# Nine-tap depthwise convolutions of a windowed-attention layer: one part of each on GpSimd instead of VectorE

## The chip, the cores and the metric

The kernel runs on one core of a Trainium2 chip. The metric is the device time of one execution in microseconds (us), from the first to the last instruction plus what lies around it. Its engines work side by side, each with its own queue of instructions in order: TensorE (PE; its weight loads are listed as PEld), VectorE (DVE), ScalarE (ACT), GpSimd (POOL) and SyncE (SP), which issues the DMAs. They wait for each other by semaphores.

## The reference

Four layers in a row, each on an image batch of 4 x 192 x 56 x 56 in float32: a convolutional attention with an MLP, a channel gate from a DCT pooling, a windowed attention with overlapping windows, and a four-direction selective scan. The change is in the third one. After its attention it computes:

```python
def _hft(x, w, b):
    a = 3.0 * x
    for s in (2, 4, 8):
        pool = x.reshape(B, C, h // s, s, ww // s, s).mean(axis=(3, 5))
        a = a - jnp.repeat(jnp.repeat(pool, s, axis=2), s, axis=3)
    return jax.nn.sigmoid(_dwconv3(a, w, b)) * x

out = _hft(_conv1x1(out, proj_w, proj_b), hft_w, hft_b)
x1 = x + out
z = jax.nn.gelu(_conv1x1(_ln_c(x1, n2g, n2b), fc1_w, fc1_b), approximate=False)
z1, z2 = jnp.split(z, 2, axis=1)
z = z1 * _dwconv3(_ln_c(z2, sgn_g, sgn_b), sg_w, sg_b)
return x1 + _conv1x1(z, fc2_w, fc2_b)
```

`_dwconv3` is a depthwise 3x3 convolution with a border of zeros: every channel with nine weights of its own. The first (the gate) has 192 channels, the second (in the MLP) 384.

## The kernel before, in words

Channels lie on partitions: 192 as two halves of 96, 384 as three parts of 128. In the third layer (`layer2` in the code) each image is cut in two ways. The attention goes by five bands of rows: `front` (layer norm, q and k), 25 `quad`s of four windows in each band (GpSimd copies the windows out into `xw` and `qw` at L1737, TensorE multiplies, VectorE adds the bias, finds the maximum and subtracts it, ScalarE takes the exponential, and VectorE adds the results into the accumulator `bacc` at L1841), and `back` (division and projection into `bp`). What follows the attention goes by seven chunks of eight rows, 28 in all. Chunk i passes through three threads of work:

- `head(i)`: VectorE makes the sums over 2, 4 and 8 pixels and the padded image `bapad`, then the gate's convolution into `bxn` (`dwconv`, L1527 the first tap with the bias, L1529 the other eight, for two halves); ScalarE a tanh (L1596), GpSimd copies two rows of `bapad` on for the next chunk (L1597), VectorE multiplies and adds (L1600, L1602), then a layer norm.
- `grow(i)`: GpSimd copies two rows of `bzpad` (L1647), TensorE expands to 768 channels, ScalarE applies the GELU; the half z2 is normed into the padded image `bzpad`, the half z1 stays in `bz`.
- `tail(i)`: the MLP's convolution of `bzpad` into `bg` (`dwconv` again, for three parts), VectorE's product with z1 (L1683), GpSimd's copy of a row of z1 (L1684), the last projection (L1692) and the sum into `bp` (L1700).

A chunk has 7 to 9 rows in `head` (7, 8, 8, 8, 8, 8, 9 in an image) and 6 to 10 in `tail` (6, 8, 8, 8, 8, 8, 10); a row is 56 pixels. So a tap of an eight-row chunk is one VectorE instruction of 448 elements for each half or part, which reads the shifted window of the padded image and the sum so far, and writes the sum.

The order of the work on PE, DVE, ACT and POOL is made while the program is built, by the class `Order`. Every thread is a generator that yields the engine and the estimated cost of its next step (`on_dve`, `on_pool` and so on, with a microsecond formula each), or a condition that must hold first. Of all threads whose next step may go, `Order.run` takes the one that could start first, with 0.05 us for each unit of the thread's place as a handicap. The outcome is one fixed queue for each engine; at run time, semaphores alone make an engine wait. A buffer kind named in `Order` is taken by `take` and given back by `done`. `gone(...)` and the `at` counters are the conditions: `head(i)` begins when `head(i - 1)` is through, `tail(i)` when `tail(i - 1)` is, `grow(i)` when the convolution of `tail(i - 2)` is.

Before the layer, the second layer's last gate scales image 3 in 14 pieces, each loaded into a buffer `xg`, scaled by ScalarE and stored again (L1184 to L1191); two such buffers exist. `front` of image 3 waits until that is over.

Of the kernel before, what the change touches and what calls it, by code (L numbers as in the profile page):

```python
# [15 lines left out]
F32 = mybir.dt.float32  # L16
AF = mybir.ActivationFunctionType
ALU = mybir.AluOpType
# [4 lines left out]
B, C, H, W = 4, 192, 56, 56  # L23
HW = H * W
HALF = 96
CH = 448
# [235 lines left out]
class Order:  # L262
# [29 lines left out]
    def take(self, kind="bank"):  # L292
        slot = min((s for s in self.kinds[kind] if s[0] is not None), key=lambda s: s[0])
        slot[0] = None
        return slot[1]
# [71 lines left out]
def on_dve(*n, takes=(), ready=None, each=0.00105):  # L367
    return "DVE", sum(0.08 + each * i for i in n), takes, None, ready
# [10 lines left out]
def on_pool(*n, each=0.0011):  # L379
    return "POOL", sum(0.2 + each * i for i in n), (), None, None  # L380


def on_sp(*takes):
    return "SP", 0.5, takes, None, None


BASE2, BASE3 = 150, 330
# [24 lines left out]
def layers01(tc, pools, x_in, packs, aps, dst):  # L412
    nc = tc.nc
# [6 lines left out]
    last = pools["2"].enter_context(tc.tile_pool(name="a_last", bufs=1, side="right"))  # L420
# [14 lines left out]
    with tc.tile_pool(name="a_stat", bufs=6) as sp:  # L435
# [3 lines left out]
        for b in range(B):  # L439
            for c in range(NCHUNK):  # L440
                t = sp.tile([HALF, 2, CH], F32, name="xs")
# [99 lines left out]
    def keep(name, shape, n, rows=128, pool=per):  # L541
        return [pool.tile([rows, *shape], F32, name=f"{name}{i}") for i in range(n)]

    def keep_att(*args):
        return keep(*args, pool=att)
# [15 lines left out]
    for t in bank_tiles:  # L561
        nc.vector.memset(t, 0.0)
    order = Order(
        nc,
        bank=bank_tiles,
        xc=xc,
        xq=xq,
        vt=keep_att("vt", [NG, 4, 64], 1, 112),
        X=keep_att("X", [WIN, 2, PADW], 4),
        sm=keep_att("sm", [WIN, W], 4),  # L570
        sd=keep_att("sd", [WIN, W], 1),
# [1 line left out]
        vb=keep_att("vb", [7, 256], 2, 112),  # L573
        ot=keep("ot", [14 * 112], 4),
        pool=keep("pool", [2, H * DCT], 1, HALF),
        xg=keep("xg", [CH], 2, HALF, last),
        hm=keep("hm", [CH], 2),
    )
    take, done = order.take, order.done
# [217 lines left out]
    parts = ((0, 16), (16, 28))  # L797
# [436 lines left out]
def layer2(tc, order, pools, src, packs, aps, dst):  # L1234
# [9 lines left out]
    nc = tc.nc  # L1244
# [11 lines left out]
    def keep(name, shape, n, rows=128):  # L1256
        return [const.tile([rows, *shape], F32, name=f"{name}{i}") for i in range(n)]
# [86 lines left out]
    p2 = ctx.enter_context(tc.tile_pool(name="b_2", bufs=1, side="right"))  # L1344
# [62 lines left out]
    def gone(*what):  # L1407
        return what[-1] < 0 or what in passed
# [107 lines left out]
                done(po)  # L1516
        at["back"] += 1

    def dwconv(parts):


        for t in range(9):
            yield on_dve(*(n * W for _, _, _, n, _, _ in parts), each=0.0012)
            for dst, pad, i, n, wt, bias in parts:
                x = pad[:, i + t // 3 : i + t // 3 + n, t % 3 : t % 3 + W]
                if t == 0:
                    nc.vector.tensor_scalar(dst, x, wt[:, 0:1], bias, ALU.mult, ALU.add)  # L1527
                else:
                    nc.vector.scalar_tensor_tensor(dst, x, wt[:, t : t + 1], dst, ALU.mult, ALU.add)  # L1529

    def rows_behind(c, n):

        return max(8 * c - n, 0), (H if c == NCHUNK - 1 else 8 * c + 8 - n)
# [3 lines left out]
    def head(i):  # L1537

        b, c = divmod(i, NCHUNK)
        y0, y1 = rows_behind(c, 1)  # L1540
        n = y1 - y0
        xn = xn2s[i % 2]
        yield lambda: at["head"] == i and at["back"] > NB * b + band_of[c] and gone("z1", i - 2)
        yield on_sp("xl")
        xt = take("xl")
        xr = xt[:HALF, :, : n * W]
        nc.sync.dma_start(xr, pixels(src[b])[:, :, y0 * W : y1 * W])

        x = pr[:HALF, :, 8 * c : 8 * c + 8]
        sums = []  # L1550
        for m in (4, 2, 1):
            xs = 7 * m
            yield on_dve(2 * m * xs, 2 * m * xs, m * xs, m * xs)
            a = p2.tile([HALF, 2, 2 * m, xs], F32, name=f"hx{m}", tag=f"hx{m}", bufs=1)
            v = x.rearrange("p h y (x r) -> p h y x r", r=2)
            for h in range(2):
                nc.vector.tensor_add(a[:, h], v[:, h, :, :, 0], v[:, h, :, :, 1])
            s = p2.tile([HALF, 2, m, xs], F32, name=f"hs{m}", tag=f"hs{m}", bufs=1)
            v = a.rearrange("p h (y r) x -> p h y r x", r=2)
            for h in range(2):  # L1560
                nc.vector.tensor_add(s[:, h], v[:, h, :, 0], v[:, h, :, 1])
            sums.append(s)
            x = s
        s2, s4, s8 = sums
        for t, u, m in ((s4, s8, 1), (s2, s4, 2)):
            yield on_dve(*[14 * m * m] * 4)
            for i_ in range(2):
                for h in range(2):
                    tv = t[:, h].rearrange("p (y r) (x s) -> p r y x s", r=2, s=2)[:, i_]
                    nc.vector.scalar_tensor_tensor(tv, bcast(u[:, h], 3, 2), 0.25, tv, ALU.mult, ALU.add)  # L1570
        yield on_dve(*[224] * 4)
        if c == 0:
            nc.gpsimd.memset(apad[:, :, 1, 1 : 1 + W], 0.0)
        for i_ in range(2):
            for h in range(2):

                out = apad[:, h, 2 + i_ : 10 : 2, 1 : 1 + W].rearrange("p y (x s) -> p y x s", s=2)
                v = pr[:HALF, h, 8 * c + i_ : 8 * c + 8 : 2].rearrange("p y (x s) -> p y x s", s=2)
                nc.vector.scalar_tensor_tensor(out, bcast(s2[:, h], 3, 2), -1.0 / 12, v, ALU.mult, ALU.add)
        gate = xn[:HALF, :, : n * W]  # L1580
        yield from dwconv(
            [
                (
                    rows2(gate[:, h]),
                    apad[:, h],
                    y0 + 1 - 8 * c,
                    n,
                    w["b96.hft_w"][:, h],
                    w["b96.hft_b"][:, h : h + 1],
                )  # L1590
                for h in range(2)
            ]
        )

        yield on_act(2 * n * W, table=GELU)
        nc.scalar.activation(gate, gate, AF.Tanh, scale=0.5)  # L1596
        nc.gpsimd.tensor_copy(apad[:, :, 0:2, 1 : 1 + W], apad[:, :, 8:10, 1 : 1 + W])  # L1597
        px = slice(y0 * W, y1 * W)
        yield on_dve(2 * n * W)
        nc.vector.scalar_tensor_tensor(gate, gate, 1.0, p[:HALF, :, px], ALU.add, ALU.mult)  # L1600
        yield on_dve(2 * n * W)
        nc.vector.scalar_tensor_tensor(p[:HALF, :, px], gate, 0.5, xr, ALU.mult, ALU.add)  # L1602
        done(xt)
        yield from layer_norm(p[:, :, px], xn[:, :, : n * W], n * W, HALF, 2, mean96)
        at["head"] += 1
# [60 lines left out]
    def tail(i):  # L1666

        b, c = divmod(i, NCHUNK)
        zpad = zpads[i % 2]
        yield lambda: at["tail"] == i and gone("z2", i)  # L1670
        y0, y1 = rows_behind(c, 2)
        n = y1 - y0
        i1 = y0 + 2 - 8 * c
        yield from dwconv(
            [
                (g[:, m, :n], zpad[:, m], i1, n, w["b128.sg_w"][:, m], w["b128.sg_b"][:, m : m + 1])
                for m in range(3)
            ]
        )
        passed.add(("conv", i))  # L1680
        yield lambda: gone("z1", i)
        yield on_dve(3 * n * W)
        nc.vector.tensor_mul(g[:, :, :n], g[:, :, :n], z1[:, :, i1 : i1 + n])  # L1683
        nc.gpsimd.tensor_copy(z1[:, :, 0], z1[:, :, 8])  # L1684
        passed.add(("product", i))
        for u, v in ((0, n),) if n <= 8 else ((0, n // 2), (n // 2, n)):
            px = slice((y0 + u) * W, (y0 + v) * W)
            for h in range(2):
                yield on_pe(3 * (v - u) * W, "bank")
                po = take()  # L1690
                for m in range(3):
                    nc.tensor.matmul(  # L1692
                        rows2(po[:HALF, : (v - u) * W]),
                        w["b128.fc2T"][:, m, HALF * h : HALF * h + HALF],
                        g[:, m, u:v],
                        start=(m == 0),
                        stop=(m == 2),
                    )
                yield on_dve((v - u) * W)
                nc.vector.scalar_tensor_tensor(  # L1700
                    p[:HALF, h, px],
                    po[:HALF, : (v - u) * W],
                    w["b96.fc2_b"][:, h : h + 1],
                    p[:HALF, h, px],
                    ALU.add,
                    ALU.add,
                )
                done(po)
            yield on_sp()
            nc.sync.dma_start(pixels(dst[b])[:, :, px], p[:HALF, :, px])  # L1710
        at["tail"] += 1
# [701 lines left out]
```

## Time and profile before

| what | before |
|---|---|
| runs | 5952.47, 5952.52, 5965.42 us; median 5952.52 |
| profiled execution | 5975.54 us |
| its span, first to last instruction | 5973.8 us |
| mean granted TensorE clock | 0.926 |
| PE busy | 4964.2 us (83%) |
| DVE busy | 4435.9 us (74%) |
| ACT busy | 2574.0 us (43%) |
| POOL busy | 1475.0 us (25%) |
| DMA, mean | 79 GB/s |

The profile is of one execution. Its groups give for each line, engine and operation the tiles (out<-in, buffer numbers left out), the shapes, the count, then the busy time in us and the mean duration in ns, then how long the engine was idle just before and what ended that. A line view gives minimum, median and maximum in ns. A timeline lists instructions in order of time, those in a row merged. A share of busy time is an average over the whole execution; the third layer's chunks fill about 1826 us in its middle, and what a step is worth there is read from that stretch alone. The span's forty slices show the stages: VectorE is below 90% in most slices of the first two layers, near 90% through the third, and GpSimd rises from 2 tenths there to 4 to 6 tenths in the fourth.

```profile
DVE  5878338446651148989989998978788888878997
POOL 0000000000000032222312212101455445445564
```

### The profile page before, as it was taken

What the parts mean: (1) busy time and instruction counts of PE and PEld (TensorE: products, weight loads), DVE (VectorE), ACT (ScalarE), POOL (GpSimd) and SP (SyncE); (2) the same over time, 40 slices, a digit from 0 to 9 for tenths busy, and PEclk for the clock granted to TensorE, in tenths of its full rate; (3) what the DMA queues carried; (4) which work ended last, traced back from release to release, by engine and by line L of the source; (5) the groups of instructions that cost most, each with busy time, mean ns of one, the idle gap of its engine ahead of it and who ended that gap; (6) DMA issues with size and microseconds to landing.
All of it is one profiled execution on the core that took longest, in us unless ns stands there. A gap on an engine that the chain in (4) does not pass through costs nothing.

```text
span 5973.8 us, 106699 instructions
## 1 busy us (share of the span) xinstructions
PE 4964.2 (83%) x42870; PEld 2374.8 (40%) x42870; DVE 4435.9 (74%) x7048; ACT 2574.0 (43%) x3977; POOL 1475.0 (25%) x1423
## 2 busy tenths in 40 slices
PE   4988998998896978778788888757898898898777
PEld 2444544554454445445445444422222222222112
DVE  5878338446651148989989998978788888878997
ACT  0122322313222236446455555435566565655544
POOL 0000000000000032222312212101455445445564
PEclk9999999999997989889899999878998999999999
DMA  6233224334324310000000000002456556556654
GB/s 177 55 73 67 60 67 95 64 91 102 66 59 98 77 52 16 15 15 21 13 20 19 16 17 20 11 20 72 125 132 155 143 129 155 146 127 149 168 148 117
DMA packets 356638, 473.82 MB, mean 79 GB/s; under 512 B 43600, under 2 KB 355408, under 8 KB 355632
## 3 DMA queue, kind: packets, MB, share of 16 engines
q1 hardware_dynamic: 356144, 466.99, 31.8%
q8 instruction: 339, 5.55, 0.4%
q14 instruction: 155, 1.27, 0.1%
HBM read 249.53 MB, written 63.17 MB: 52 GB/s over the span
## 4 chain that ended last, share of the span: by engine, by line
PE 48%; DVE 37%; issue 5%; ACT 4%; DMA 3%; POOL 1%; SPq 0%; DVEq 0%; POOLq 0%; ACTq 0%
PE bank L723 6%; DVE bg L1529 6%; PE bank L2051 5%; PE bank L1024 4%; PE bank L1009 4%; DVE bxn L1529 4%; DVE st L2290 3%; PE bank L2008 2%; PE bank L656 2%; PE bank L2268 2%; DVE X L691 2%; PE bank L2313 2%; DVE bank L2274 2%; PE bank L1692 2%; PE bank L600 1%
## 5 line engine op out<-in xcount | busy, mean ns | idle before, releaser
L2297 POOL TENSOR_TENSOR da<-st,bc 128x448 f32<-128x448 f32 x672 | 857.4, 1281 | 850.0 <-DVE st L2290 634.7
L723 PE MATMUL bank<-X,wu 64*49 64x392 f32 x6720 | 616.8, 512 | 89.0 <-DVE X L702 86.0
L2290 DVE TENSOR_TENSOR_SCAN st<-da,st,bank 128x448 f32<-128x448 f32 x576 | 647.7, 1134 | 0.7 <-ACT da L2243 0.7
L830 POOL TENSOR_TENSOR attn<-attn,rs 112x1568 f32<-112x1568 f32 (+1 forms) x24 | 67.1, 2796 | 1728.8 <-DVE rs L828 1299.1
L349 ACT ACT_TABLE_LOAD x375 | 481.1, 1283 | 6.7
L2274 DVE TENSOR_TENSOR bank<-bank,bc 128x448 f32<-128x448 f32 x672 | 382.9, 618 | 115.2 <-PE bank L2268 115.0
L2243 ACT ACTIVATE da<-da,a_neg 128x448 f32<-128x448 f32 x672 | 413.7, 658 | 111.4 <-DMA da<-dt 108.8
L1529 DVE SCALAR_TENSOR_TENSOR bg<-bzpad,w_b,bg 128x448 f32<-128x448 f32 (+2 forms) x672 | 424.2, 686 | 0.0
L723 PEld LDWEIGHTS bank<-X,wu 64*49 64x49 f32 x6720 | 248.7, 124 | 421.2 <-issue 370.4
L2313 PE MATMUL bank<-da,w_c 128*32 128x448 f32 x1344 | 356.0, 578 | 71.6 <-POOL da L2297 65.4
L2268 PE MATMUL bank<-du,w_c 32*128 32x448 f32 x1344 | 261.5, 628 | 102.0 <-DVE du L2258 61.6
L1618 PE MATMUL bank<-bxn,w_b 128*128 128x448 f32 (+2 forms) x672 | 294.4, 566 | 23.0 <-DVE bxn L1400 16.5
L2051 PE MATMUL bank<-pad,diag 128*96 128x448 f32 (+2 forms) x756 | 297.4, 543 | 2.3 <-ACT pad L2019 2.3
L1024 PE MATMUL bank<-hm,w_a 128*96 128x448 f32 x672 | 284.4, 554 | 16.6 <-ACT hm L1018 16.6
L1018 ACT ACTIVATE hm<-bank,w_a 128x448 f32<-128x448 f32 x168 | 106.5, 634 | 430.3 <-PE bank L1009 422.9
L1529 DVE SCALAR_TENSOR_TENSOR bxn<-bapad,w_b,bxn 96x448 f32<-96x448 f32 (+2 forms) x448 | 289.1, 688 | 0.0
L1009 PE MATMUL bank<-xc,w_a 128*128 128x448 f32 x672 | 282.2, 549 | 0.6 <-DVE xc L990 0.6
L1394 PE MATMUL bank<-bsq,b_mean 128*96 128x336 f32 (+7 forms) x424 | 188.0, 578 | 85.5 <-ACT bsq L1389 84.7
L1737 POOL COPY qw<-bq 96x256 f32<-96x256 f32 x200 | 153.5, 794 | 385.3 <-PE bank L1767 323.1
L670 ACT ACTIVATE q<-bank,qk_bias,qk_scale 128x280 f32<-128x280 f32 (+2 forms) x216 | 117.2, 545 | 297.6 <-PE bank L656 259.7
L2008 PE MATMUL bank<-row,w_c 128*96 128x448 f32 x448 | 205.6, 591 | 38.0 <-DVE row L1974 37.8
L1692 PE MATMUL bank<-bg,w_b 128*96 128x448 f32 (+2 forms) x384 | 161.7, 566 | 84.3 <-DVE bg L1683 46.7
(323 smaller groups left out, 9314.8 us busy)
## 6 DMA issues: line engine op xcount, KB each, us to landing
da<-dt SPq DMA_DIRECT2D x672, 224.0 KB
vb<-vmem SPq DMA_DIRECT2D x576, 98.0 KB
bc<-prod SPq DMA_DIRECT2D x224, 224.0 KB
xq<-x SPq DMA_DIRECT2D x132, 210.0 KB
xc<-x SPq DMA_DIRECT2D x56, 336.0 KB
row<-x SPq DMA_DIRECT2D x56, 336.0 KB
xs<-x SPq DMA_DIRECT2D x28, 336.0 KB
vmem<-vt SPq DMA_DIRECT2D x56, 168.0 KB
```

The costliest lines, as they stand in the source:

```text
L349: self.nc.scalar.preload_act_table_set(table)
L723: nc.tensor.matmul(pm[a][outs[i], : WIN * W].rearrange("p (y x) -> p y x", x=W), wu[halves[a], k, dx], xt[halves[a], :, i, dx : dx + W], s ...
L1009: nc.tensor.matmul(ph[:, :CH], w["a128.c1T"][:, k, 128 * m : 128 * m + 128], xt[:, k], start=(k == 0), stop=(k == 1),)
L1024: nc.tensor.matmul(acc[h][:HALF, :CH], w["a128.c2T"][:, m, HALF * h : HALF * h + HALF], hm, start=(m == 0), stop=(m == 5),)
L1529: nc.vector.scalar_tensor_tensor(dst, x, wt[:, t : t + 1], dst, ALU.mult, ALU.add)
L2051: nc.tensor.matmul(rows2(pc[:HALF, : n * W]), diag[:, h, t], pad[:, h, at + t // 3 : at + t // 3 + n, t % 3 : t % 3 + W], start=(t == 0), ...
L2243: nc.scalar.activation(da, da, AF.Exp, scale=a_neg[:, k, g : g + 1])
L2268: nc.tensor.matmul(tiles[j][:, :SCH], w["c96.rep"][r], du[r], start=True, stop=True)
L2274: nc.vector.tensor_mul(tiles[j][:, :SCH], tiles[j][:, :SCH], b_)
L2290: nc.vector.tensor_tensor_scan(sts[j][:, r], da[:, r], tiles[j][:, :SCH][:, r], first, ALU.mult, ALU.add)
L2297: nc.gpsimd.tensor_mul(da, sts[j], c_)
L2313: nc.tensor.matmul(py[32 * j : 32 * j + 32, :SCH], w["c128.sum"], das[j], start=True, stop=True)
```

## The change

Of the parts that `dwconv` is given, the last one (one of the gate's two halves, one of the MLP's three parts) leaves VectorE's loop and becomes a thread of its own, `share`, for GpSimd. There a tap is two instructions, a product into a scratch tile `tap` and an addition out of it; the first tap is still one. `tap` holds five rows, so a tap is cut in two: rows 0 to 4 and the rest. There is one `tap` for both convolutions. VectorE's loop makes the other parts as before, and `dwconv` then waits, in the planned order, until the share is through. To make room for `tap`, the last gate's buffer `xg` exists once instead of twice. `head` and `tail` pass a name for the share ("h" or "t" and the chunk), which sets its place in the order.

```diff
-        xg=keep("xg", [CH], 2, HALF, last),
+        xg=keep("xg", [CH], 1, HALF, last),
...
-    def dwconv(parts):
+    tap = p2.tile([128, 5, W], F32, name="tap")
+
+    def dwconv(parts, tag):
+        *parts, other = parts
+        shares.add(("pool", *tag))
+
+        def share():
+            for t in range(9):
+                dst, pad, i, n, wt, bias = other
+                x = pad[:, i + t // 3 : i + t // 3 + n, t % 3 : t % 3 + W]
+                if t == 0:
+                    yield on_pool(n * W, each=0.0012)
+                    nc.gpsimd.tensor_scalar(dst, x, wt[:, 0:1], bias, ALU.mult, ALU.add)
+                    continue
+                yield on_pool(*[n * W // 2] * 4, each=0.0017)
+                for y in range(0, n, 5):
+                    e = min(y + 5, n)
+                    v = tap[: x.shape[0], : e - y]
+                    nc.gpsimd.tensor_scalar(v, x[:, y:e], wt[:, t : t + 1], None, ALU.mult)
+                    nc.gpsimd.tensor_add(dst[:, y:e], dst[:, y:e], v)
+            shares.discard(("pool", *tag))
+
+        order.add(BASE2 + 25 / 7 * tag[1] + (8 if tag[0] == "h" else 12), share(), "2")
         for t in range(9):
             yield on_dve(*(n * W for _, _, _, n, _, _ in parts), each=0.0012)
             for dst, pad, i, n, wt, bias in parts:
...
+        yield lambda: ("pool", *tag) not in shares
+
+    shares = set()
...
                 for h in range(2)
-            ]
+            ],
+            ("h", i),
         )
...
                 for m in range(3)
-            ]
+            ],
+            ("t", i),
         )
```

## The prediction

> **What bounds the kernel now.** The change touches one stage, the third layer. I first took the line view for L1529, the nine-tap convolution: it runs from 2244.4 to 4066.1 us. Then the busy time of each engine in that stretch (columns: length, then PE, PEld, DVE, ACT, POOL busy with instruction counts, granted PE clock, DMA share, GB/s):
>
> ```profile
> 2244.00:4070.00 1826.00, 1449.94 (x14041) 824.02 (x14040) 1645.14 (x3176) 916.73 (x1356) 407.08 (x557) 0.90 0.06 17
> ```
>
> DVE is busy 1645 of 1826 us, 90%; PE 79%; POOL 22%. The chain of waits of this stretch says the same: L1529 alone holds 32% of it (bg 20.2%, bxn 11.8%). So DVE sets the pace here, and the convolutions are 709 us of its time, with 74 us for the first taps at L1527 (the same view, cut to these two lines). Moving part of this to an engine that is idle 78% of the time looks like a gain. The next views ask what POOL would pay. The groups of instructions in the stretch, DVE and POOL:
>
> ```profile
> L1529 DVE SCALAR_TENSOR_TENSOR bg<-bzpad,w_b,bg 128x448 f32<-128x448 f32 x480 | 301.8, 683 | 0.0
> L1529 DVE SCALAR_TENSOR_TENSOR bxn<-bapad,w_b,bxn 96x448 f32<-96x448 f32 x320 | 206.6, 687 | 0.0
> ...
> L1737 POOL COPY qw<-bq 96x256 f32<-96x256 f32 x180 | 146.1, 838 | 371.0 <-PE bank L1767 316.8 <-ACT bq L1456 45.8 <-PE bank L1798 8.1
> L1737 POOL COPY xw<-bxn 128x256 f32<-128x256 f32 x180 | 114.8, 668 | 204.9 <-PE bank L1747 129.4 <-DVE bxn L1400 64.3 <-issue 10.6
> L1470 POOL MEMSET bacc<- 96x3472 f32 x17 | 50.9, 2995 | 187.8 <-PE bank L1502 151.8 <-DVE bacc L1482 29.3 <-DVE hx L1557 6.7
> ```
>
> The line view of L1737 gives what the mean hides: minimum, median, maximum.
>
> ```profile
> L1737 POOL COPY qw<-bq x200: 390/401/21300, 2180.5 to 3816.1; 96x256 f32<-96x256 f32 x100
> ```
>
> A copy of 0.39 us has a mean of 0.84 and once took 21.3 us. The timeline shows that one, POOL first and then DVE beside it:
>
> ```profile
> 2962.57 22.77 POOL L1737 COPY qw<-bq 96x256 f32<-96x256 f32 x3 [3.75 <-ACT bq L1456]
> 2985.28 3.06 POOL L1737 COPY xw<-bxn 128x256 f32<-128x256 f32 x2
> 2988.30 0.74 POOL L1737 COPY qw<-bq 96x256 f32<-96x256 f32 x2
> ```
> ```profile
> 2980.14 1.86 DVE L1529 SCALAR_TENSOR_TENSOR bg<-bzpad,w_b,bg 128x448 f32<-128x448 f32 x3
> 2981.93 1.08 DVE L1600 SCALAR_TENSOR_TENSOR bxn<-bxn,bp 96x896 f32<-96x896 f32 x1
> 2982.93 2.14 DVE L1529 SCALAR_TENSOR_TENSOR bg<-bzpad,w_b,bg 128x448 f32<-128x448 f32 x3
> ...
> 2987.67 1.07 DVE L1780 TENSOR_TENSOR e<-bank,w_b 128x256 f32<-128x256 f32 x3
> ```
>
> While DVE ran taps without a break (they read two tiles in SBUF), POOL's copy stood still; when POOL got in, the three taps took 2.14 instead of 1.86 us; and the moment DVE read PSUM (`bank`, L1780), the copies ran at 0.37 each. The opposite order stands in the fourth layer, at 4558 us:
>
> ```profile
> 4558.39 4.41 POOL L2297 TENSOR_TENSOR da<-st,bc 128x448 f32<-128x448 f32 x4
> ```
> ```profile
> 4561.14 2.13 DVE L2258 TENSOR_TENSOR du<-dt,u 96x448 f32<-96x448 f32 x1
> ```
>
> DVE's product of two SBUF tiles, 0.61 us elsewhere, waited until POOL's products were through. MEMSETs (L1470, 2.99 us each, 2.99 at best) and DVE's PSUM reads (L1841, 0.41) keep their time. So these two engines shut each other out exactly for the kind of work that is moved.
>
> **What goes.** A third of the bg taps and half of the bxn taps: 0.4 of the 1120 rows of L1529 (224 + 224) and 56 of 140 of L1527. In busy time 0.4 x 709 = 283 and 0.4 x 74 = 30: 313 us off DVE, which has 1332 left. Its two-SBUF work in the stretch (L1529 709; L1791 90, L1683 43, and L1557, L1561, L1570, L1579, L1482, L1494, L1600, L1602, L2044 together 219) falls from 1061 to 778. Where the gate's chain runs alone on DVE, each tap now needs the tap just before it and loses the 0.08 us overlap (0.67 long, 0.60 apart): at most 224 x 0.08 = 18 us; taken as 0, since the timeline shows the chains of bg and bxn interleaved.
>
> **What comes.** 56 shares (28 chunks, gate and MLP). Each is one tensor_scalar and eight taps of two pieces (5 rows and the rest), a product and an add each: 33 instructions, 1848 in all. The rows of an image are 56 by 56, so a tap is 8 x 3136 = 25,088 elements per partition over the run.
> Adds: L2297 takes 1.134 us for 448 elements and L2132 2.07 for 896, so 2.09 ns an element + 0.197 us. Eight taps: 200,704 x 2.09 ns + 896 x 0.197 = 596 us.
> Products with a per-partition factor: no row shows one on POOL. Below, MEMSETs (0.191 us for 112, 0.381 for 336: 0.85 ns + 0.096): 257 us. Above, priced as an add: 596. Nearest are the copies, which read and write one tile (0.322 for 168, 0.459 for 336: 0.815 ns + 0.185): 329 us, the value taken. First taps alike: 31 (27 to 63).
> Undisturbed sum 956 us (880 to 1255), 17.1 per share. For every DVE microsecond removed POOL gets three.
>
> **The wait in front of each.** POOL's 482 copies in the stretch took 335 us (their eight groups summed); at their minimum they would take 187. That is 0.31 us of waiting per read, with DVE's two-SBUF work filling 58% of the time. Afterwards 778 of about 2000 us, 39%, gives 0.31 x 39/58 = 0.21 us. The bounds: 0 (every read falls beside DVE's PSUM work) and 0.6 (a whole tap before each). New reads: 1848 x 0.21 = 388; the old copies: 482 x 0.21 = 101. Each new instruction depends on the one before it (product into `tap`, add out of it), so the 0.05 us by which back-to-back POOL work overlaps is lost: 92.
> POOL in the stretch: 956 + 388 + 92 + 187 + 101 + 79 (memsets) = 1803 us. DVE: 1332, plus what POOL's reads cost it. A copy of 0.39 us cost a tap 0.14; an instruction that is longer by d costs it 0.14 + d, so a tap of 5 + 3 rows (0.41, 0.32, 0.78, 0.55) costs 1.0 us if all four collide, 56 x 8 x 1.0 = 450 us, and at about half of that DVE has 1332 + 225 = 1557. **POOL becomes the fullest engine**, and all that stands in its queue comes late: the quads' copies qw and xw, on which PE waits at L1747 and L1767, the row copies of bapad and bzpad, and through the new share the tanh at L1596 and the product at L1683.
>
> In sentences by themselves: the Trainium skill, "SBUF — State Buffer", section "Who interferes with whom", says that a DVE instruction with two SBUF inputs contends with a GpSimd instruction that reads SBUF, and that whoever issues first has the pair for the whole instruction while the other fully blocks. The rows agree on who contends, but a copy of 0.39 us delayed a tap by only 0.14. By the rule taken whole, 778 + 956 + 187 us cannot overlap: 1921, already above 1826, and nothing could be gained.
>
> **The other edits.** With one `xg` buffer each load of the last gate waits for the store before it. The 14 pieces run from 2135 to 2189 us beside the start of the layer; SP issues xl loads in between. At best 0; at worst a landing of some 2 us more on each, 28. Taken as 5, because only image 3 needs the result, hundreds of us later, and only a few xl loads stand behind them. The last chunk's 17.2 us of bg taps (4049.64) become 20 to 25 us of share with nothing else running: inside the fill below.
>
> **Sum.** The fullest engine fills 90% of the stretch today. POOL at 90%: 1803 / 0.90 = 2003 us, 177 more than 1826; with xg 182. The profiled execution took 5975.5 us (span 5973.8), so 6157.5; the median of the runs is 0.99615 of that execution, which gives **6134 us**. At a fill of 0.95: 1898, +77 with xg. With products as dear as adds: (1803 + 299) / 0.90 = 2336, +515.
>
> **Rivals.**
> (1) Faster: POOL finds its turns. It is decided by the wait per POOL read. POOL breaks even at 1826 x 0.90 = 1643 us, and 956 + 187 + 79 are fixed, so 421 us remain for 2330 reads: below 0.18 us each, gap included, POOL keeps up and DVE's relief counts: (1332 + 185) / 0.90 = 1686 us, -140 at full, about half of it likely: 5975.5 + 5 - 70 = 5910, scaled 5888. For it: the copies around 2984 us alternate with taps, and 42% of DVE's time left reads PSUM or one tile. Against: the measured wait is 0.31 today.
> (2) Much slower: long runs shut the other engine out, as at 2962. If only half of DVE's 554 us of one-input work lies beside POOL: 778 + 277 + 956 + 187 + 92 = 2290, +464: 6420. For it: the 21.3 us copy. Against: DVE's runs become shorter by 40%.
> (3) Nothing measurable: relief and waits cancel, 5952. The order in which engines get work is planned with 0.58 us per POOL piece and no shutting out, so what does not fit shows as waits, not as a different plan.
>
> **Chances.** Forecast (+60 to +300) 0.57; much slower 0.15; nothing measurable or a little on either side 0.06; faster 0.22. Faster by over 0.3% (18 us, about what a measurement of this kernel can tell from no change) 0.22, within 0.06, slower 0.72. Range 5880 to 6420: its low end lies just under the likely half of rival 1, its high end is rival 2; what lies beyond (rival 1 in full, 5818; products as dear as adds, 6465) is left out with less than 2 in 10.
>
> **What would show it.** In the changed profile, POOL in the third layer's stretch near 1800 us and 85 to 95% full; the adds at 0.8 to 1.0 us on average against 0.78 and 0.55 undisturbed, with maxima of many us; DVE near 1550 and no longer the fullest, with ACT's tanh (L1596 before) and DVE's product (L1683 before) waiting for POOL; L1737 still far above 0.39; L1529's mean above 0.68. It is wrong if POOL's mean add is at its undisturbed price while DVE's two-SBUF work goes on, or if products cost as much as adds.

## The result, and the profile after

The changed kernel takes **6682.09 us** (median of 4 runs, 6679.76 to 6688.12) against 5958.97 before in the same comparison: ratio **1.1205**, 95% interval 1.1186 to 1.1224. Slower was forecast, with 6134; the loss is four times as large and lies above the range.

In the profiles, 700 of the 704 us between the two lie in the third layer's stretch. Counted from the first pixel sum of `head` to the last product of `tail`, the stretch is 2228 to 4069 us before and 2236 to 4777 after: 1841 and 2541 us. What follows it takes 1905 and 1901. The busy time of each engine in the stretch that answers to the one shown (length; PE, PEld, DVE, ACT, POOL busy; granted clock, DMA share, GB/s):

```profile
2244.00:4780.00 2536.00, 1513.16 (x14178) 854.95 (x14178) 1487.10 (x2705) 927.82 (x1371) 1994.01 (x2413) 0.79 0.05 13
```

DVE is at 59% where it was at 90%, POOL at 79% where it was at 22%: the fullest engine has changed, as forecast. The granted clock of TensorE fell too, from 0.90 to 0.79, but that isn't the loss: PE's busy time rose from 1450 to 1513 us only, and PE has 1000 us free here. The page's groups for the moved work (L1539 is the product, L1540 the add, L1551 what DVE kept of the taps):

```profile
L1539 POOL TENSOR_SCALAR tap<-bzpad,w_b 128x280 f32<-128x280 f32 x448 | 462.5, 1032 | 35.2
L1539 POOL TENSOR_SCALAR tap<-bapad,w_b 96x280 f32<-96x280 f32 x448 | 445.2, 994 | 38.0
...
L1540 POOL TENSOR_TENSOR bg<-bg,tap 128x280 f32<-128x280 f32 x448 | 354.4, 791 | 37.4
L1540 POOL TENSOR_TENSOR bxn<-bxn,tap 96x280 f32<-96x280 f32 x448 | 338.6, 756 | 37.3
...
L1551 DVE SCALAR_TENSOR_TENSOR bg<-bzpad,w_b,bg 128x448 f32<-128x448 f32 (+2 forms) x448 | 338.8, 803 | 0.0
```

The products took 908 us, more than the adds with 693. The timeline shows them where nothing disturbs them, POOL's first tap of a gate at 3085 us and then two pieces of an MLP tap:

```profile
3085.55 0.71 POOL L1533 TENSOR_SCALAR bxn<-bapad,w_b 96x448 f32<-96x448 f32 x1
3086.24 0.98 POOL L1539 TENSOR_SCALAR tap<-bzpad,w_b 128x280 f32<-128x280 f32 x1
3087.30 0.77 POOL L1540 TENSOR_TENSOR bg<-bg,tap 128x280 f32<-128x280 f32 x1
3088.17 0.71 POOL L1539 TENSOR_SCALAR tap<-bzpad,w_b 128x168 f32<-128x168 f32 x1
3088.96 0.54 POOL L1540 TENSOR_TENSOR bg<-bg,tap 128x168 f32<-128x168 f32 x1
```

A product of 280 elements takes 0.98 us and an add 0.77, while the first tap, with 448 elements and two operations, takes 0.71. Between the pieces lie 0.08 to 0.10 us each. Elsewhere the two engines shut each other out as in the profile before. At the last chunk POOL's first tap stands for 12.51 us, and DVE's timeline shows why:

```profile
4729.80 12.51 POOL L1533 TENSOR_SCALAR bg<-bzpad,w_b 128x560 f32<-128x560 f32 x1 [24.20 <-ACT bzpad L1679]
4742.29 1.34 POOL L1539 TENSOR_SCALAR tap<-bzpad,w_b 128x280 f32<-128x280 f32 x1
```
```profile
4729.80 11.48 DVE L1551 SCALAR_TENSOR_TENSOR bg<-bzpad,w_b,bg 128x560 f32<-128x560 f32 x16
4741.20 0.50 DVE L2069 TENSOR_SCALAR u<-pad,w_c 96x448 f32<-96x448 f32 x1
```

Sixteen taps on DVE run without a break, and POOL's instruction ends 1.0 us after the last of them. The waits of the stretch (engine, tile and line that wait, <- for whom: us in total, times, longest) show who is late now:

```profile
PE bank L1719 <- DVE bg L1710: 485.4, 28, 40.0
DVE bg L1710 <- POOL bg L1540: 460.7, 28, 32.1
PEld bank L1719 <- DVE bg L1710: 403.1, 23, 40.7
ACT bxn L1622 <- POOL bxn L1540: 353.7, 27, 31.8
```

In every one of the 28 chunks DVE stands at the product L1710 for the share, 461 us in all, and all that is queued behind it on DVE stands too.

### The profile page after: what moved, and what is told of

Its sections match the earlier page's. It is cut to its first block, busy times and chain, and to the rows that moved or that the text cites. A ratio compares the mean times of both kernels' runs of the same rounds, so it can differ in the third digit from the quotient of the medians.

```text
span 6677.9 us, 107844 instructions
## 1 busy us (share of the span) xinstructions
PE 5012.3 (75%) x42870; PEld 2403.1 (36%) x42870; DVE 4263.5 (64%) x6544; ACT 2577.1 (39%) x3980; POOL 3060.8 (46%) x3271
## 4 chain that ended last, share of the span: by engine, by line
PE 41%; POOL 28%; DVE 17%; issue 5%; ACT 5%; DMA 4%; SPq 0%; POOLq 0%; DVEq 0%; ACTq 0%
POOL tap L1539 13%; PE bank L723 6%; POOL bg L1540 5%; POOL bxn L1540 5%; PE bank L2078 4%; PE bank L1024 4%; PE bank L1009 4%; DVE st L2317 3%; PE bank L656 2%; PE bank L2035 2%; PE bank L2340 2%; PE bank L2295 2%; DVE bank L2301 2%; DVE X L691 2%; PE bank L1719 1%
## 5 line engine op out<-in xcount | busy, mean ns | idle before, releaser
L1719 PE MATMUL bank<-bg,w_b 128*96 128x448 f32 (+2 forms) x384 | 196.4, 666 | 485.4 <-DVE bg L1710 485.4
L1539 POOL TENSOR_SCALAR tap<-bzpad,w_b 128x280 f32<-128x280 f32 x448 | 462.5, 1032 | 35.2
L1539 POOL TENSOR_SCALAR tap<-bapad,w_b 96x280 f32<-96x280 f32 x448 | 445.2, 994 | 38.0
L1540 POOL TENSOR_TENSOR bg<-bg,tap 128x280 f32<-128x280 f32 x448 | 354.4, 791 | 37.4
L1540 POOL TENSOR_TENSOR bxn<-bxn,tap 96x280 f32<-96x280 f32 x448 | 338.6, 756 | 37.3
L1710 DVE TENSOR_TENSOR bg<-bg,bz 128x1344 f32<-128x1344 f32 (+2 forms) x28 | 46.0, 1643 | 460.7 <-POOL bg L1540 460.7
L1551 DVE SCALAR_TENSOR_TENSOR bg<-bzpad,w_b,bg 128x448 f32<-128x448 f32 (+2 forms) x448 | 338.8, 803 | 0.0
L1719 PEld LDWEIGHTS bank<-bg,w_b 128*96 128x96 f32 x384 | 79.3, 216 | 581.2 <-DVE bg L1710 403.1
```

Of the source, the lines that this page charges most:

```text
L1539: nc.gpsimd.tensor_scalar(v, x[:, y:e], wt[:, t : t + 1], None, ALU.mult)
L1540: nc.gpsimd.tensor_add(dst[:, y:e], dst[:, y:e], v)
```

## The experiments

Three theories. **Occupancy**: POOL's own instructions fill its queue and set the pace. **Port**: the time goes where DVE's and POOL's reads shut each other out. **Order**: the planner was told 2.3 us for a POOL tap that takes 4, so it puts what depends on the share too early in DVE's queue. Some later expectations name a fourth, **chain**: the moved part comes late from any other engine, whichever it is. In runs 1, 2, 7, 12 and 15 most of POOL's taps are left out, so these kernels don't compute the layer; they only price a part of the change. The runs with one time only were made beside runs of the kernel before at 5966 to 5972 us. One time can lie some 20 us off: the twelve times of run 13 reach from 5951.67 to 5996.54.

**1. No taps on POOL but the first.**

```diff
-                for y in range(0, n, 5):
-                    ...
```


> Leaves out taps 2 to 9 of GpSimd's part (its first tap stays); the planned order of all other work is that of the changed kernel. What VectorE's relief is worth if GpSimd's share costs nothing. Occupancy theory (GpSimd's own queue sets the pace) and port theory (the two engines shutting each other out sets it) both expect the stretch to fall to VectorE's 1332 us at 90% full, 1480 us instead of 2536: about 5630 us, below the kernel before. If the planned order itself is at fault, it stays above 5950.

5810.63 us, not 5630. The stretch is 1671 us, not 1480: DVE 1387 us (83%), PE 1411 (84%). The relief exists, but less of it than expected reaches the time. That PE and the waits between the engines take over is read from these two fills, not shown by a run.

**2. MEMSETs in place of products and adds.**

```diff
+                for _ in range(n):
+                    nc.gpsimd.memset(dst[:, :5], 0.0)
```


> Replaces products and adds of each GpSimd tap by as many MEMSETs of five rows as the tap has rows (leaves taps 2 to 9 of that part out). 8 x (0.334 + 0.08 gap) = 3.3 us a tap, as long as the undisturbed 0.98 + 0.77 + 0.70 + 0.54 + gaps 0.36 = 3.35, but write-only, so it shuts nobody out. Occupancy theory: within 150 us of the changed kernel's 6680, since only the 365 us of waiting in front of GpSimd's reads goes, and part of that is in old copies. Port theory: 6250 or less, with the taps of VectorE back from 0.80 to 0.67 us.

6347.45 us: between the two. Against run 1, 537 us come from POOL being occupied by instructions that read nothing (stretch 2204); the reads bring another 335. DVE's taps are back at a median of 0.67. Neither theory is enough alone.

**3 and 4. The product with a second operation.**

```diff
-nc.gpsimd.tensor_scalar(v, x[:, y:e], wt[:, t : t + 1], None, ALU.mult)
+nc.gpsimd.tensor_scalar(v, x[:, y:e], wt[:, t : t + 1], 0.0, ALU.mult, ALU.add)
```


> The product gets a second operation, plus a column of zeros, like the first tap, which took 0.71 us for 448 elements where the plain product takes 0.98 for 280. If the form sets the price: 0.50 for 280 and 0.36 for 168, 0.82 us less a tap, 367 less on GpSimd; occupancy theory then expects 367 / 0.857 = 430 less, 6250 us; port theory about half of that. If the price is that of any product into a second tile, nothing changes: 6680.

> As e3_two_ops with the constant 0.0 in place of the column: tells whether the second operation or the kind of its operand makes the first tap cheap. 6250 us if the operation, 6680 if the operand.

6490.69 us with a column of zeros, 6374.11 with the constant. The line view of the product in the changed kernel (minimum, median, maximum in ns), and of the same line with the constant:

```profile
L1539 POOL TENSOR_SCALAR tap<-bzpad,w_b x448: 424/984/8056, 2321.8 to 4773.2; 128x280 f32<-128x280 f32 x86, 128x168 f32<-128x168 f32 x53, 128x56 f32<-128x56 f32 x11
```
```profile
L1539 POOL TENSOR_SCALAR tap<-bzpad,w_b x448: 310/499/7570, 2323.9 to 4475.3; 128x280 f32<-128x280 f32 x86, 128x168 f32<-128x168 f32 x53, 128x56 f32<-128x56 f32 x11
```

An addition of zero halves the product: 0.50 instead of 0.98 us. So the second operation makes the product cheap, of whichever kind its operand; the column costs 0.07 more than the constant (0.57). 308 us of the loss were the price of the one-operation form against the form with the constant. Both times lie above the occupancy theory's 6250: the first is near what half of the 430 would give (6465), the second between. Of the 117 us between the two runs, the column's 0.07 on each of 896 products is some 65.

**5 and 6. The right prices for the planner**, without and with the cheap product.

```diff
-yield on_pool(n * W, each=0.0012)
+yield on_pool(n * W, each=0.0025)
-yield on_pool(*[n * W // 2] * 4, each=0.0017)
+yield on_pool(*[n * W // 2] * 4, each=0.0035)   (0.0027 with the constant)
```


> The changed kernel with the planner told what a GpSimd tap really took (about 4.0 us for eight rows, waits and gaps included, instead of 2.3; first tap 1.3 instead of 0.7); every instruction is the same, only the planned order moves. Order theory (VectorE stands at the product L1710 and at the tanh's successors because the plan puts them too early, 461 us): VectorE has other work meanwhile, GpSimd's fill rises from 0.86 to 0.95, 2172 / 0.95 = 2286 us of stretch, about 6430. Occupancy theory (GpSimd is the pace whatever the order): 6600 to 6690.

> Product with the constant as second operation, which took 0.50 instead of 0.98 us for 280 elements, and the prices that this form showed (3.2 us a tap). Order theory: 200 us below the 6374 of the same form with the old prices. Occupancy theory: within 80 us of it, 6300 to 6400.

6455.25 and 6207.78 us: 227 and 166 less with the same instructions. The order theory, with 6430 and 6174, holds for that part. The stretch of the first, and its wait at the product:

```profile
2248.00:4574.00 2326.00, 1542.05 (x14307) 865.12 (x14306) 1547.34 (x2727) 965.46 (x1398) 2019.97 (x2423) 0.82 0.05 14
```
```profile
DVE bg L1710 <- POOL bg L1540: 130.6, 26, 19.9
```

DVE's wait for the share falls from 461 to 131 us, and POOL is busy 2020 of 2326 us. With the gaps between dependent instructions (144 us of pauses under 0.15 us) it is 93% full, and POOL's share makes up 61% of the chain of waits: now POOL really sets the pace.

**7. MEMSETs with the right prices.** The edit of run 2 with `each=0.0028`.

> The MEMSETs in place of products and adds (taps 2 to 9 of GpSimd's part left out), with the planner told their 3.3 us a tap: GpSimd as occupied as in the changed kernel's undisturbed sum, nobody shut out, and the order right. Occupancy theory: GpSimd's 1620 us at 0.87 full, as after the right prices in e5, 1860 us of stretch, about 6000. Port theory: VectorE sets the pace again, under 5900, as with the first tap only (5811).

6146.69 us, above both figures.

```profile
2251.00:4243.00 1992.00, 1479.28 (x14302) 838.06 (x14301) 1402.09 (x2727) 937.48 (x1379) 1596.09 (x4213) 0.88 0.06 16
```

What it shows is occupancy: POOL 1596 us busy and 189 of gaps in 1992, 90% full, DVE at 70% with its taps at 0.69 on average, as in the kernel before. I had left the gaps out of the expectation.

**8 to 11. Half of the move.** The gate alone or the MLP alone on POOL, the cheap product, old prices and then right ones.

```diff
+        moved = tag[0] == "h"          ("t" for the MLP)
+        if moved:
             *parts, other = parts
```


> Only the gate's half on GpSimd, the MLP's convolution whole on VectorE; product with the constant. GpSimd's busy time in the stretch falls to about 426 + 600 = 1030 us, so it no longer is the fullest; VectorE has 1645 - 160 = 1485 plus some 120 of waiting. Occupancy theory: near the kernel before, 5900 to 6000. Port theory: half of the loss stays, 6150 or more.

> The mirror of e6_gate_imm: only a third of the MLP's channels on GpSimd. Occupancy theory: 5900 to 6000, as there. Port theory: 6150 or more. If the loop head to head (tanh behind the share) weighs more than the product behind it, this one is the faster of the two.

> The gate's half alone on GpSimd, product with the constant, prices as measured (3.2 us a tap). Order theory: as between e4 and e8, the waits of VectorE at the share's end shrink: 6126 less some 80 to 120, 6010 to 6050. If what is left there is the port alone, it stays within 40 of 6126. To beat the kernel before it would have to fall below 5935.

> The third of the MLP alone on GpSimd, product with the constant, prices as measured. Order theory: 6187 less 80 to 120, 6070 to 6110; port theory: within 40 of 6187.

6125.86 us for the gate, between the two theories, and 6187.46 for the MLP, where the port theory put it; that the MLP alone would be the faster one didn't come true. With right prices 6080.05 for the MLP and, timed four times, 6037.92 for the gate, both as the order theory had it: ratio 1.011 (1.0086 to 1.0133) for the gate. Its stretch:

```profile
2249.00:4152.00 1903.00, 1495.17 (x14302) 857.14 (x14301) 1617.04 (x2972) 905.66 (x1356) 1127.66 (x1499) 0.87 0.06 17
```

Even this best case loses, although POOL is only 59% busy (1127 of 1903 us) and its prices are right. How full POOL is doesn't explain that.

**12. The same half, write-only.** Run 9's order with MEMSETs of the same length.

```diff
+                for _ in range(n - 2):
+                    nc.gpsimd.memset(dst[:, :5], 0.0)
```


> e9 with its products and adds replaced by MEMSETs of the same length in the same planned order (taps 2 to 9 of the gate's GpSimd half left out): GpSimd as busy, but write-only. Port theory: VectorE's busy time falls from 1617 to about 1500 and the time by 80 to 130, 5910 to 5960. Chain theory: within 30 of e9's 6038.

5906.66 us, 131 below run 9 (6038), in the same planned order: the port theory holds, and the chain theory's 30 is far exceeded. The stretch, then DVE's taps in run 9 and here:

```profile
2237.00:4001.00 1764.00, 1436.37 (x14302) 821.89 (x14301) 1520.19 (x2971) 905.16 (x1357) 944.71 (x1947) 0.91 0.06 18
```

```profile
L1554 DVE SCALAR_TENSOR_TENSOR bg<-bzpad,w_b,bg 128x448 f32<-128x448 f32 (+2 forms) x672 | 471.1, 756 | 0.0
L1554 DVE SCALAR_TENSOR_TENSOR bxn<-bapad,w_b,bxn 96x448 f32<-96x448 f32 (+2 forms) x224 | 181.0, 808 | 4.4
```
```profile
L1551 DVE SCALAR_TENSOR_TENSOR bg<-bzpad,w_b,bg 128x448 f32<-128x448 f32 (+2 forms) x672 | 423.4, 685 | 0.0
L1551 DVE SCALAR_TENSOR_TENSOR bxn<-bapad,w_b,bxn 96x448 f32<-96x448 f32 (+2 forms) x224 | 156.7, 700 | 4.4
```

0.07 to 0.11 us on each of 896 taps, 72 us on this line alone; DVE's busy time is 1617 against 1520 us. POOL's falls as well, from 1127 to 945 us, since nothing stands in front of a MEMSET; the 131 us are both sides together. Without the reads the half is worth 59 us against the kernel before, and they take back more than that.

One cost of the reads is left in both runs, since POOL's first tap still reads. In run 9 it stood like this four times, once in each image, for 21.35 us instead of 0.71:

```profile
2409.57 21.36 POOL L1535 TENSOR_SCALAR bxn<-bapad,w_b 96x448 f32<-96x448 f32 x1 [4.90 <-DVE bapad L1608]
```
```profile
2429.75 0.67 DVE L1554 SCALAR_TENSOR_TENSOR bxn<-bapad,w_b,bxn 96x448 f32<-96x448 f32 x1
2430.35 0.73 DVE L1872 TENSOR_TENSOR bacc<-bacc,bank 96x256 f32<-96x256 f32 x2
```

DVE ran 32 taps meanwhile, with one first tap and one product among them, and POOL's instruction ended 0.58 us after DVE turned to PSUM (`bank`). Run 12 has the same four. Right prices don't prevent that; what these 83 us of POOL's time cost wasn't tested.

**13. The same half on TensorE and ScalarE.** ScalarE scales the identity by a tap's weights, TensorE sums nine taps in PSUM.

```diff
+nc.scalar.activation(dg[:, t % 3], ident[:HALF, :HALF], AF.Copy, scale=wt[:, t : t + 1])
...
+nc.tensor.matmul(rows2(pc[:HALF, : n * W]), dg[:, u % 3], x, start=(u == 0), stop=(u == 8))
```


> The gate's half leaves VectorE as in e9, but goes to engines that do not touch VectorE's port: ScalarE scales the identity by the weights of a tap (9 x some 0.3 us a chunk), TensorE sums the nine taps in PSUM (9 x some 0.55), ScalarE writes them out with the bias. TensorE gets 28 x 5 = 140 us more, 1460 + 140 of a stretch of about 1800. Port theory of what e9 still loses: VectorE keeps its 160 us of relief, stretch 1841 less 30 to 90, 5890 to 5950. Chain theory (the part comes late from any other engine): as e9, about 6040.

5972.32 us, ratio 1.0014 (1.0002 to 1.0026): above its expectation, and level with before.

```profile
2241.00:4078.00 1837.00, 1600.04 (x14801) 885.05 (x14799) 1514.00 (x2961) 986.78 (x1628) 420.64 (x574) 0.95 0.06 17
```

DVE keeps its relief here (1514 us), but PE goes from 79 to 87%; its nine products a chunk are 218 us of busy time, not 140. This kernel also has the one `xg` buffer, which run 14 prices at 18 us; less these, an estimate of 5954 would lie just above the expectation. That PE's fullness eats the rest of the relief is argued from this line, not shown by a run.

**14. One `xg` buffer in the kernel before.**

```diff
-        xg=keep("xg", [CH], 2, HALF, last),
+        xg=keep("xg", [CH], 1, HALF, last),
```


> The kernel before with one xg buffer in place of two, nothing else. Every theory: 0 to 28 us more, 5 expected; the ratio to the kernel before within 1.000 and 1.005.

Ratio 1.0031 (1.0016 to 1.0045): 18 us. In its profile the chunks' stretch begins at 2245 us instead of 2228.

**15. Run 1 planned for what it is.** The share's later taps are left out of the plan too.

```diff
-            for t in range(9):
-                ...
+            yield on_pool(n * W, each=0.0012)
+            nc.gpsimd.tensor_scalar(dst, x, wt[:, 0:1], bias, ALU.mult, ALU.add)
```


> As e1 (taps 2 to 9 of GpSimd's part left out) with the planner told that they are not there: the most that the move could have given. e1 was planned with 19 us shares that never ran. Both theories: 5700 to 5800; if the stretch is held by TensorE and the chains rather than by VectorE, no better than e1's 5811.

5728.80 us: the most that the move had to give is 237 us, 4%. The stretch before and here:

```profile
2228.00:4069.00 1841.00, 1463.63 (x14297) 834.29 (x14295) 1656.98 (x3214) 923.86 (x1369) 416.52 (x575) 0.90 0.06 17
```
```profile
2240.00:3834.00 1594.00, 1394.40 (x14293) 803.60 (x14291) 1371.46 (x2710) 906.37 (x1358) 475.89 (x628) 0.95 0.07 20
```

DVE has 285 us less, and PE is the fullest engine, at 87%.

**16. First taps on ScalarE**, in the kernel before, for all five parts.

```diff
-                    nc.vector.tensor_scalar(dst, x, wt[:, 0:1], bias, ALU.mult, ALU.add)
+                    nc.scalar.activation(dst, x, AF.Identity, bias=bias, scale=wt[:, 0:1])
```


> The kernel before (two xg, no scratch tile) with the first tap of all five parts on ScalarE, as one activation with scale and bias, in place of VectorE's tensor_scalar: 74 us off VectorE's 1657 in the stretch, 28 x 5 x some 0.6 = 84 more on ScalarE's 924, no GpSimd, no reads by way of the shared port. Port theory: most of the relief stays, by e15's proportion (237 + 18 us for 313) some 50 to 60: 5905 to 5920. Chain theory: the detour over ScalarE eats it, 5950 to 5990.

**5869.13 us, ratio 0.9835 (0.9818 to 0.9851)**: faster than both kernels, by more than its expectation, with a stretch of 1756 us instead of 1841.

```profile
L1530 ACT ACTIVATE bg<-bzpad,w_b 128x448 f32<-128x448 f32 (+2 forms) x84 | 57.7, 753 | 0.0
L1530 ACT ACTIVATE bxn<-bapad,w_b 96x448 f32<-96x448 f32 (+2 forms) x56 | 39.6, 754 | 74.8 <-DVE bapad L1582 74.8
```

DVE's busy time falls by 65 us, from 1657 to 1592; at the same fill of 90% that is 72 us of stretch. The stretch lost 85 us and the whole kernel 95: the rest isn't explained, the planned order is another one too. Runs 13 and 16 both spare DVE without POOL, and only the second pays: ScalarE has 984 us of work in its 1756, TensorE had 1600 in 1837. That the room on the taking engine decides is argued from these two runs.

**The sum.** Run 15 (237 below before), then POOL occupied with the right prices (run 7, +418), then its reads (run 5, +308), then the low prices (the changed kernel, +227): -237 + 418 + 308 + 227 = 716, and 6682 - 5966 = 716. The order in which the steps are taken has a part in their sizes. The MEMSETs of run 7 are as long as the dear products, so the price of that form (308 us in run 4) is spread over these steps. And runs 5 and 7 are each planned with their own price, 3.9 and 3.3 us a tap, so the 308 of the third step hold a difference of plan besides the reads.

## Why the prediction was wrong, point by point

- *The size.* The forecast was 177 us of stretch more than 1826, and it became 710 more (2536 in the window shown). POOL's sum was 369 us too small, which at the fill of 90% is 410; the fill was 86%, which is the other 123.
- *What goes.* Nearly right: 313 us were foretold, and without POOL's taps DVE had 1372 against 1657 us, 285 less. It was worth 237. Where the 28 went wasn't traced.
- *Products.* **This step failed, and it is the larger part of the miss.** I took 329 us by the copies and put the upper end at the price of an add, 596. They took 0.98, 0.84, 0.70, 0.56 and 0.42 us for 280, 224, 168, 112 and 56 elements: 480 x 0.98 + 320 x 0.70 + 32 x (0.84 + 0.56 + 0.42) = 753 us undisturbed. An instruction that reads one tile was held to cost no more than one that reads two; on POOL in this form it costs 1.27 times as much. The prediction's own sign of being wrong, products as dear as adds, came true. Run 4 shows the weight of this step in the time: with products at half the price the kernel is 308 us faster.
- *Adds.* 596 foretold; 480 x 0.77 + 320 x 0.54 + 32 x (0.65 + 0.42 + 0.30) = 586. Right.
- *Waits and gaps.* At each form's undisturbed duration POOL's stretch would be 1657 us; it lasted 2022. 365 us over 2330 reads are 0.16 each, against 0.21 foretold (489 in all). The gaps were 150, not 92. The mechanism was right: run 12 shows it. (The nine smaller lines in the 1061 us of two-tile work add up to 247, not 219; the 0.21 stays.)
- *POOL's sum.* 1803 foretold, 2022 + 150 = 2172 found, with the durations added up (1994 us where overlaps count once): 435 more of work, 424 of it the products, 124 less of waits, 58 more of gaps.
- *Fill.* 90% was carried over from DVE; it was 2172 / 2536 = 86%. I had seen that the planner prices a POOL piece at 0.58 us and wrote that this shows as waits and not as a different plan. The prices cost 227 us (run 5), and with right ones POOL fills 93%. This step failed too, as the smaller part: it carried over the fill of an engine whose plan was right to a queue whose plan is wrong.
- *xg.* 5 us taken, 18 measured, inside the bound of 28.
- *DVE.* 1557 foretold, 1487 found; taps at 0.80 instead of 0.68 us on average, as the list of signs said.
- *Rival 1* named 0.18 us per read, gap included, as the point from which POOL keeps up. Found were 0.16 + 0.06 = 0.22. It would have been close with cheap products; run 6 has these and right prices, and still lost 4%.
- *Rival 2* came nearest in size, but mostly for another reason: long runs did shut POOL out (12.51 us), while the waits in all were smaller than even the main sum foretold.

The Trainium skill, "GPSIMD Engine Reference", section "Engine selection", calls one-input operations roughly line-rate. The two-operation product fits (0.50 for 280, 0.40 for 168: 0.8 ns an element; VectorE's own one-input instruction at L2069 above took 0.50 for 448, at most 1.1 ns); the one-operation product of the changed kernel doesn't (0.98 and 0.70: 2.5 ns). The measurement decides.

## What to carry to other kernels

Before work goes to an idle engine, ask what it will cost there in the very form in which it will run, and take as the upper bound something dearer than the nearest row when no row shows the form. Look in the profile for instructions of the target engine that are far above their own minimum: what stood beside them is what the move will collide with. Where a planner or a hand-written order fixes the queues, its price for the moved work must be the measured one, waits included, or the consumer stands at the head of its queue.

## What the runs showed of the hardware

- GpSimd's tensor_scalar with one operation (multiply by a per-partition column) took 0.98 us for 280 elements; with `+ 0.0` as a second operation 0.50, with a column of zeros 0.57. The cause wasn't looked into.
- GpSimd's reads of SBUF and VectorE's instructions with two SBUF inputs shut each other out, and not for one instruction only: a read of 0.71 us stood for 21.36 behind 32 taps. In the other direction VectorE's taps rose to 0.77 us on average in run 9. MEMSETs in the same place and of the same length cost them nothing: 0.69 in run 12, as in the kernel before.
